# Layer 2's last projection on Trainium2: seven block products for eight

## The chip, the cores and the metric

The kernel runs on one core of one Trainium2 chip. The metric is the device time of one execution in microseconds; lower is better. TensorE does the matrix products (PE in the profile, its weight loads PEld), VectorE the elementwise work (DVE), ScalarE the activations and copies (ACT), GpSimd a few small operations (POOL), and SyncE (SP) issues most transfers. All data is fp32.

## The reference, cut to what matters

Four graph layers run one after the other on 32 independent batch elements, each with 512 nodes of 128 features and a 512x512 matrix `adj`. Every layer is `x = x + layer(relu(layernorm(x)))`. The change lies in layer 2, which has four sublayers of its own:

```
def _layer(nodes, adj, ws, bs, wd, bd, wn, bn, wu, bu):
    src = nodes @ ws + bs
    src_agg = jnp.einsum('bjv,bij->biv', src, _l2norm(adj, 2))
    dst = nodes @ wd + bd
    dst_agg = jnp.einsum('bjv,bji->biv', dst, _l2norm(adj, 1))
    self_rep = nodes @ wn + bn
    upd = jnp.concatenate([src_agg, self_rep, dst_agg], axis=2)
    return jnp.tanh(upd @ wu + bu)
...
for i in range(4):
    if i < 2:
        stashed.append(fpass)                                        # f0, f1
    elif i == 2:
        fpass = concatenate([fpass, stashed[1]], axis=2)             # f2, f1
    else:
        fpass = concatenate([fpass, stashed[1], stashed[0]], axis=2) # f3, f1, f0
    fpass = _layer(fpass, adj, *params[i])
```

The last sublayer (`i == 3`) projects three features, f3, f1 and f0, to `src` and `dst`: per element a 512x384 matrix times a 384x256 matrix. Two thirds of that product, the f1 and f0 rows of the weights, need nothing that is made after the first sublayer.

## The kernel before: the parts that matter

The program is a list of operations. Each names its engine, an estimated duration, and the buffers that it reads and writes. A list scheduler (`Plan.order`) then works out the order of instructions on every engine ahead of time, across all 32 elements, so that several elements are in flight at once. An operation's urgency comes from a due time for its element, `batch * PERIOD`, less the work that still follows. Buffers come from a fixed number of places: 8 PSUM banks, 32 places of 2 KiB a partition (`s2`), 6 of 4 KiB (`s4`), 10 of 8 KiB (`s8`).

```
plan = Plan(sb, psum, {"bank": 8, "s2": 32, "s4": 6, "s8": 10}, {"bank": 1, "s2": 7, "s4": 0, "s8": 0})
...
def t_mm(n):
    return n * 0.001675 + 0.004
def mm(ps, out_of, lhs, rhs, n, start, stop, reads, later=0.0):
    op("PE", t_mm(n), lambda: nc.tensor.matmul(out_of(ps.ap()), lhs(), rhs(), start=start, stop=stop),
       reads, [ps], later=later)
```

The last dictionary says how many places an element that isn't the oldest must leave free. All ordinary matmuls are issued in `mm`, so all of them carry the line L289 in the profile; the names of the tiles tell them apart. The helper for the source and destination projections works on two blocks of 128 nodes at a time, adds up the features in one PSUM bank, and adds the bias on VectorE (L490):

```
def paired_rows(nodes, wcols, wbuf, bias, bbuf, col):
    sd = buf("s4", (P, NC, 2 * D), "sd")
    for h in range(NC // 2):
        ps = plan.bank("sd")
        for j in range(2):
            c = 2 * h + j
            for k, nk in enumerate(nodes):
                mm(ps, lambda t, j=j: t[:, j * 2 * D:(j + 1) * 2 * D],
                   lambda nk=nk, c=c: nk.ap()[:, c * P:(c + 1) * P],
                   lambda k=k: wt(wcols + k * 2 * D, 2 * D), 2 * D, k == 0, k == len(nodes) - 1, [nk, wbuf])
        op("DVE", t_tt(N), lambda ps=ps, h=h: nc.vector.tensor_add(
            sd.ap()[:, 2 * h:2 * h + 2, :], ps.ap().rearrange("p (j v) -> p j v", j=2),
            along(bias, col, 2 * D, 2)), [ps, bbuf], [(sd, {2 * h, 2 * h + 1})])
    return sd
```

Here `P` and `D` are 128, `N` is 512 and `NC` is 4. A feature is held transposed, 128 partitions (features) by 512 columns (nodes); a 128-column block of it is the stationary operand, and the weights (128x256: source beside destination) are the moving one. The four sublayers use it like this. The weights have the update weights `wu` multiplied in once at the start ("fold"), so the aggregations add straight into the bank that the tanh reads:

```
for i, (wsd, wn) in enumerate(W_L2):
    sd = paired_rows(f, wsd, W2F, rf_sb, RF, i * 2 * D)
    ps = plan.bank("agg")
    linear_t(ps, [wn + k * D for k in range(len(f))], f, W2F, stop=False)
    for m, lo in ((aT, 0), (a, D)):
        for c in range(NC):
            mm(ps, lambda t: t, lambda c=c, lo=lo, sd=sd: sd.ap()[:, c, lo:lo + D], lambda c=c, m=m: m.ap()[:, c, :], N,
               False, lo > 0 and c == NC - 1, [(sd, {c}), (m, {c})])
    f_new = buf("s2", name=f"f{i + 1}")
    op("ACT", ...tanh of ps with bias...)
    stashed.append(f_new)
    f = {0: [f_new], 1: [f_new, stashed[1]], 2: [f_new, stashed[1], stashed[0]], 3: [f_new]}[i]
```

Of the kernel before, what the change touches and what calls it, by code (L numbers as in the profile page):

```python
# [13 lines left out]
F32 = mybir.dt.float32  # L14
# [4 lines left out]
P = 128  # L19
# [4 lines left out]
L2_CHUNKS = (1, 1, 2, 3)  # L24
PERIOD = 30.0
ENDING = 6.0
SMALL = 16


# [32 lines left out]
R_L0, R_L1_IO, R_L1_UPD, R_L3_MSG, R_L3_G, R_L3_HRZ = (k * D for k in (0, 1, 3, 4, 5, 9))  # L62
R_COLS = 11 * D

# [159 lines left out]
def gnn_stack(  # L224
# [15 lines left out]
    dram = ctx.enter_context(tc.tile_pool(name="dram", bufs=1, space=bass.MemoryType.DRAM))  # L240
    plan = Plan(sb, psum, {"bank": 8, "s2": 32, "s4": 6, "s8": 10}, {"bank": 1, "s2": 7, "s4": 0, "s8": 0})

# [3 lines left out]
    rf_sb = const.tile([P, len(L2_CHUNKS) * 2 * D], F32, name="rf_sb")  # L246
    cf_sb = const.tile([P, len(L2_CHUNKS)], F32, name="cf_sb")
    ident = const.tile([P, P], F32, name="ident")
    neg_half = const.tile([P, 2 * NC], F32, name="neg_half")
# [8 lines left out]
    def t_mm(n):  # L258
        return n * 0.001675 + 0.004

# [15 lines left out]
    def op(*args, **kwargs):  # L276
        return plan.op(*args, **kwargs)

    def const_buf(name, ap):
        b = Buf(plan, name, name, None)  # L280
        b.tile, b.slot = ap, 0
        return b

    W1, W2F, W3, CS, RS, RF, CF, ID, NH = (const_buf(n, t) for n, t in (
        ("w1", w_sb), ("w2", w_sb), ("w3", w_sb), ("c_sb", c_sb), ("r_sb", r_sb), ("rf_sb", rf_sb),
        ("cf_sb", cf_sb), ("ident", ident), ("neg_half", neg_half)))

    def mm(ps, out_of, lhs, rhs, n, start, stop, reads, later=0.0):
        op("PE", t_mm(n), lambda: nc.tensor.matmul(out_of(ps.ap()), lhs(), rhs(), start=start, stop=stop),  # L289
           reads, [ps], later=later)  # L290

    def setup():
# [5 lines left out]

        def spread(lo, hi):
            return lambda: nc.sync.dma_start(  # L300
                r_sb[:, lo:hi], bass.AP(tensor=brow.tensor, offset=brow.offset + lo, ap=[[0, P], [1, hi - lo]]))

# [7 lines left out]
        op("SP", 0.5, spread(R_L3_MSG, R_COLS), [], [(RS, {2})], kb=(R_COLS - R_L3_MSG) / 2)  # L310
        op("DVE", 0.4, lambda: nc.vector.tensor_add(r_sb[:, R_L3_G:R_L3_G + 2 * D], r_sb[:, R_L3_G:R_L3_G + 2 * D],
                                                    r_sb[:, R_L3_HRZ:R_L3_HRZ + 2 * D]), [(RS, {2})], [(RS, {2})])
        raws = []
# [12 lines left out]
        for i, (k, (proj, upd)) in enumerate(zip(L2_CHUNKS, RAW_L2, strict=True)):  # L326
# [23 lines left out]
            else:  # L350
# [4 lines left out]
            op("ACT", t_act(2 * D), lambda ps=ps, i=i: nc.scalar.copy(  # L355
                rf_sb[:, i * 2 * D:(i + 1) * 2 * D], ps.ap()[:, :2 * D]), [ps], [RF])

    def program(b):
# [119 lines left out]

        def paired_rows(nodes, wcols, wbuf, bias, bbuf, col):

            sd = buf("s4", (P, NC, 2 * D), "sd")
            for h in range(NC // 2):
                ps = plan.bank("sd")
                for j in range(2):
                    c = 2 * h + j
                    for k, nk in enumerate(nodes):
                        mm(ps, lambda t, j=j: t[:, j * 2 * D:(j + 1) * 2 * D],
                           lambda nk=nk, c=c: nk.ap()[:, c * P:(c + 1) * P],
                           lambda k=k: wt(wcols + k * 2 * D, 2 * D), 2 * D, k == 0, k == len(nodes) - 1, [nk, wbuf])
                op("DVE", t_tt(N), lambda ps=ps, h=h: nc.vector.tensor_add(  # L490
                    sd.ap()[:, 2 * h:2 * h + 2, :], ps.ap().rearrange("p (j v) -> p j v", j=2),
                    along(bias, col, 2 * D, 2)), [ps, bbuf], [(sd, {2 * h, 2 * h + 1})])
            return sd

        def tt(dst, fn, n, reads, engine="DVE"):
# [56 lines left out]
        for h in range(2):  # L552
            s, part = slice(2 * h, 2 * h + 2), {2 * h, 2 * h + 1}
            op("ACT", t_act(N), lambda s=s: nc.scalar.activation(rep.ap()[:, s, :], io.ap()[:, s, :], AF.Exp), [(io, part)], [(rep, part)])
            op("DVE", t_ts(N), lambda s=s: nc.vector.tensor_scalar(rep.ap()[:, s, :], rep.ap()[:, s, :], 1.0, -1.0, op0=ALU.min, op1=ALU.add),
               [(rep, part)], [(rep, part)])
            op("DVE", t_tt(N), lambda s=s: nc.vector.tensor_max(rep.ap()[:, s, :], rep.ap()[:, s, :], io.ap()[:, s, :]),  # L557
               [(rep, part), (io, part)], [(rep, part)])
        psi = plan.bank("agg")
# [48 lines left out]
        f0 = transposed(h2, "f0")  # L608
        f, stashed = [f0], [f0]
        for i, (wsd, wn) in enumerate(W_L2):  # L610
            sd = paired_rows(f, wsd, W2F, rf_sb, RF, i * 2 * D)
            ps = plan.bank("agg")
            linear_t(ps, [wn + k * D for k in range(len(f))], f, W2F, stop=False)
            for m, lo in ((aT, 0), (a, D)):
                for c in range(NC):
                    mm(ps, lambda t: t, lambda c=c, lo=lo, sd=sd: sd.ap()[:, c, lo:lo + D], lambda c=c, m=m: m.ap()[:, c, :], N,
                       False, lo > 0 and c == NC - 1, [(sd, {c}), (m, {c})])
            f_new = buf("s2", name=f"f{i + 1}")
            op("ACT", t_act(N, 1), lambda ps=ps, i=i, f_new=f_new: nc.scalar.activation(f_new.ap(), ps.ap(), AF.Tanh, bias=cf_sb[:, i:i + 1]),  # L619
               [ps, CF], [f_new])  # L620
            stashed.append(f_new)
            f = {0: [f_new], 1: [f_new, stashed[1]], 2: [f_new, stashed[1], stashed[0]], 3: [f_new]}[i]
        x3 = buf("s2", rows_shape, "xr")
# [27 lines left out]
        g = buf("s8", (P, NC, 4 * D), "g")  # L651
        for c in range(NC):
            ps = plan.bank("gate")
            blk = slice(c * P, (c + 1) * P)
            for m, lo, n, col, start, stop in ((h3T, 3, 1, W_L3_HH + 2 * D, True, True), (h3T, 0, 2, W_L3_HH, True, False),
                                               (mT, 0, 2, W_L3_IH, False, True), (mT, 2, 1, W_L3_IH + 2 * D, True, True)):
                mm(ps, lambda t, lo=lo, n=n: t[:, lo * D:(lo + n) * D], lambda m=m, blk=blk: m.ap()[:, blk],
                   lambda col=col, n=n: wt(col, n * D), n * D, start, stop, [m, W3], later=0.7 * c)
            op("DVE", t_tt(N), lambda ps=ps, c=c: nc.vector.tensor_add(g.ap()[:, c, :], ps.ap(), r_sb[:, R_L3_G:R_L3_G + 4 * D]),  # L659
               [ps, RS], [(g, {c})])  # L660


        u, n, q, w, xo = (buf("s2", rows_shape, k) for k in ("u", "n", "q", "w", "xo"))
        at_end = b >= B - 2
        side, side_engine = (nc.gpsimd, "POOL") if at_end else (nc.vector, "DVE")
        w1 = 1 if at_end else 2
        for k in range(0, NC, w1):
            s, part, cols = slice(k, k + w1), set(range(k, k + w1)), 2 * D * w1
            op("ACT", t_act(cols), lambda s=s: nc.scalar.activation(g.ap()[:, s, :2 * D], g.ap()[:, s, :2 * D], AF.Tanh, scale=0.5),  # L669
               [(g, part)], [(g, part)])  # L670
        w2 = 1 if at_end else NC
        for k in range(0, NC, w2):
            s, part, cols = slice(k, k + w2), set(range(k, k + w2)), w2 * D

            def step(dst, fn, reads, engine="DVE"):
                op(engine, t_tt(cols) if engine == "DVE" else t_pool(cols), fn, [(r, part) for r in reads], [(dst, part)])

            step(u, lambda s=s: nc.vector.scalar_tensor_tensor(u.ap()[:, s, :], g.ap()[:, s, 0:D], 1.0, g.ap()[:, s, 3 * D:], op0=ALU.add, op1=ALU.mult), [g])
            step(u, lambda s=s: nc.vector.scalar_tensor_tensor(u.ap()[:, s, :], u.ap()[:, s, :], 0.5, g.ap()[:, s, 2 * D:3 * D], op0=ALU.mult, op1=ALU.add), [u, g])
            op("ACT", t_act(cols), lambda s=s: nc.scalar.activation(n.ap()[:, s, :], u.ap()[:, s, :], AF.Tanh), [(u, part)], [(n, part)])  # L680
            op("ACT", t_act(cols), lambda s=s: nc.scalar.activation(w.ap()[:, s, :], g.ap()[:, s, D:2 * D], AF.Copy, scale=-0.5, bias=0.5), [(g, part)], [(w, part)])
            op("ACT", t_act(cols), lambda s=s: nc.scalar.activation(q.ap()[:, s, :], g.ap()[:, s, D:2 * D], AF.Copy, scale=0.5, bias=0.5), [(g, part)], [(q, part)])
            step(q, lambda s=s: side.tensor_tensor(q.ap()[:, s, :], q.ap()[:, s, :], h3.ap()[:, s, :], op=ALU.mult), [q, h3], side_engine)
# [55 lines left out]
```

## Time and profile before

| | us |
|---|---|
| device time, median of 3 runs | 2353.84 (2353.79 to 2356.74) |
| span of the profiled execution | 2352.6 |
| PE busy | 2321.2 |
| DVE busy | 1123.3 |
| ACT busy | 923.2 |

In the profile, a group of instructions is one line of the kernel, an engine, an operation and its tiles (output<-inputs). Times are microseconds unless marked ns. TensorE instructions are pipelined: a matmul's recorded length reaches into the next one's, so the distance between the starts of two matmuls is its price, not its length. Each fp32 matmul appears as two records.

### The profile page before, as it was taken

What the parts mean: (1) busy time and instruction counts of PE and PEld (TensorE: products, weight loads), DVE (VectorE), ACT (ScalarE), POOL (GpSimd) and SP (SyncE); (2) the same over time, 40 slices, a digit from 0 to 9 for tenths busy, and PEclk for the clock granted to TensorE, in tenths of its full rate; (3) what the DMA queues carried; (4) which work ended last, traced back from release to release, by engine and by line L of the source; (5) the groups of instructions that cost most, each with busy time, mean ns of one, the idle gap of its engine ahead of it and who ended that gap; (6) DMA issues with size and microseconds to landing.
All of it is one profiled execution on the core that took longest, in us unless ns stands there. A gap on an engine that the chain in (4) does not pass through costs nothing.

```text
span 2352.6 us, 24187 instructions
## 1 busy us (share of the span) xinstructions
PE 2321.2 (99%) x8466; PEld 1426.5 (61%) x8466; DVE 1123.3 (48%) x2917; ACT 923.2 (39%) x2018; POOL 282.0 (12%) x218
## 2 busy tenths in 40 slices
PE   6999999999999999999999999999999999999998
PEld 4665566566666565665666665656665666656655
DVE  4344444555445555445554445554455544454523
ACT  7424233443334443334443344433344333344312
POOL 3100011111011110011110111110111101111001
PEclk9999999999999999999999999999999999999999
DMA  6112212322313332223223133322233321332000
GB/s 239 59 54 72 72 52 92 108 86 88 99 56 104 90 99 90 75 78 108 90 90 99 50 103 91 98 90 82 72 107 90 98 91 55 98 107 72 17 10 9
DMA packets 127128, 196.36 MB, mean 83 GB/s; under 512 B 18336, under 2 KB 75040, under 8 KB 127008
## 3 DMA queue, kind: packets, MB, share of 16 engines
q1 hardware_dynamic: 126720, 194.71, 27.0%
q8 instruction: 66, 1.08, 0.2%
q14 instruction: 54, 0.44, 0.1%
q10 hardware_dynamic: 288, 0.13, 0.0%
HBM read 157.95 MB, written 36.83 MB: 83 GB/s over the span
## 4 chain that ended last, share of the span: by engine, by line
PE 94%; DVE 2%; ACT 2%; DMA 1%; issue 0%; POOL 0%; SPq 0%; DVEq 0%; POOLq 0%; ACTq 0%
PE ps_agg L289 62%; PE ps_sd L289 18%; PE ps_gate L289 7%; PE ps_upd L289 3%; PE ps_msg L289 1%; PE ps_lin L289 1%; PE ps_node L289 1%; ACT h L417 1%; POOL sc L405 0%; DMA a<-in_adj 0%; ACT sq L581 0%; DVE bn L389 0%; SPq L435 0%; DVE g L659 0%; DMA spaced<-bounce 0%
## 5 line engine op out<-in xcount | busy, mean ns | idle before, releaser
L289 PE MATMUL ps_agg<-aT,sd 128*128 128x512 f32 x1024 | 521.2, 593 | 0.0
L289 PE MATMUL ps_agg<-a,sd 128*128 128x512 f32 x1024 | 501.1, 592 | 0.0
L289 PE MATMUL ps_sd<-w_sb,f 128*128 128x256 f32 x1792 | 484.2, 381 | 1.0 <-ACT f L455 0.8
L490 DVE TENSOR_TENSOR sd<-ps_sd,rf_sb 128x512 f32<-128x512 f32 x256 | 175.9, 687 | 606.7 <-PE ps_sd L289 606.7
L289 PEld LDWEIGHTS ps_sd<-w_sb,f 128*128 128x128 f32 x1792 | 327.1, 191 | 172.8 <-issue 134.0
L405 POOL TENSOR_TENSOR sc<-v,neg_half 128x4 f32<-128x4 f32 (+1 forms) x128 | 180.1, 1408 | 2020.1 <-DVE v L392 1384.0
L417 ACT ACTIVATE h<-xr,nb,sc 128x128 f32<-128x128 f32 x384 | 157.9, 482 | 556.8 <-DVE nb L413 556.6
L289 PEld LDWEIGHTS ps_agg<-a,sd 128*128 128x128 f32 x1024 | 185.4, 191 | 164.3 <-issue 155.3
L289 PEld LDWEIGHTS ps_agg<-aT,sd 128*128 128x128 f32 x1024 | 187.1, 191 | 84.4 <-issue 56.9
L289 PE MATMUL ps_agg<-f,w_sb 128*128 128x512 f32 x448 | 229.7, 594 | 0.0
L619 ACT ACTIVATE f<-ps_agg,cf_sb 128x512 f32<-128x512 f32 x128 | 87.2, 681 | 132.0 <-PE ps_agg L289 131.9
L289 PE MATMUL ps_agg<-aT,rep 128*128 128x512 f32 x256 | 131.4, 595 | 3.6 <-DVE rep L557 3.6
L289 PEld LDWEIGHTS ps_gate<-w_sb,mT 128*128 128x128 f32 x512 | 95.3, 190 | 61.6 <-issue 55.0
L426 DVE STREAM_TRANSPOSE blk<-h 128x512 f32<-128x512 f32 x81 | 57.6, 711 | 154.8 <-ACT h L417 154.8
L289 PE MATMUL ps_agg<-a,rep 128*128 128x512 f32 x256 | 130.7, 592 | 0.0
L289 PE MATMUL ps_agg<-aT,msg 128*128 128x512 f32 x256 | 125.9, 592 | 0.0
L289 PE MATMUL ps_gate<-w_sb,mT 128*128 128x256 f32 (+1 forms) x512 | 123.1, 326 | 0.0
L289 PEld LDWEIGHTS ps_gate<-w_sb,hT 128*128 128x128 f32 x512 | 91.0, 190 | 49.8 <-issue 43.5
L289 PE MATMUL ps_gate<-w_sb,hT 128*128 128x128 f32 (+1 forms) x512 | 119.0, 327 | 0.0
L289 PE MATMUL ps_agg<-aT,h 128*128 128x256 f32 (+2 forms) x384 | 108.8, 380 | 0.0
L603 DVE TENSOR_TENSOR aT<-aT,rows 128x512 f32<-128x512 f32 x128 | 87.8, 687 | 35.4 <-PE ps_agg L289 33.8
L669 ACT ACTIVATE g<-g 128x512 f32<-128x512 f32 (+1 forms) x68 | 41.1, 605 | 156.1 <-DVE g L659 156.1
(101 smaller groups left out, 2724.6 us busy)
## 6 DMA issues: line engine op xcount, KB each, us to landing
aT<-in_adjt SPq DMA_DIRECT2D x124, 512.0 KB, 4.8
a<-in_adj SPq DMA_DIRECT2D x62, 512.0 KB, 4.6
turn_turned<-blk SPq DMA_DIRECT2D x324, 64.0 KB, 1.8
turned<-turn_turned SPq DMA_DIRECT2D x81, 256.0 KB, 2.6
spaced<-bounce SPq DMA_DIRECT2D x32, 512.0 KB, 4.1
x<-in_x SPq DMA_DIRECT2D x32, 256.0 KB, 2.9
out<-xo SPq DMA_DIRECT2D x30, 256.0 KB, 3.0
turn_f4r<-blk SPq DMA_DIRECT2D x108, 64.0 KB, 2.3
```

The source lines that it names most:

```text
L289: op("PE", t_mm(n), lambda: nc.tensor.matmul(out_of(ps.ap()), lhs(), rhs(), start=start, stop=stop), reads, [ps], later=later)
L405: op("POOL", t_pow(n), lambda: nc.gpsimd.tensor_tensor(inv.ap()[:, :n], v8.ap()[:, :n], neg_half[:, :n], op=ALU.pow), [v8, NH], [(inv, {0})])
L417: op("ACT", t_act(D, 2), lambda c=c: nc.scalar.activation(h.ap()[:, c, :], xin.ap()[:, c, :], AF.Relu, bias=nb.ap()[:, c:c + 1], scale=inv ...
L426: op("DVE", t_tt(N), lambda: nc.vector.transpose(blk.ap().rearrange("p b (c r) -> p c b r", c=NC), m.ap().rearrange("p c (b s) -> p c b s" ...
L490: op("DVE", t_tt(N), lambda ps=ps, h=h: nc.vector.tensor_add(sd.ap()[:, 2 * h:2 * h + 2, :], ps.ap().rearrange("p (j v) -> p j v", j=2), a ...
L603: op("DVE", t_tt(N), lambda m=m, c=c, s=s: nc.vector.tensor_mul(m.ap()[:, c, :], m.ap()[:, c, :], rows.ap()[:, s, :]), [(m, {c}), rows], [ ...
L619: op("ACT", t_act(N, 1), lambda ps=ps, i=i, f_new=f_new: nc.scalar.activation(f_new.ap(), ps.ap(), AF.Tanh, bias=cf_sb[:, i:i + 1]), [ps, ...
L669: op("ACT", t_act(cols), lambda s=s: nc.scalar.activation(g.ap()[:, s, :2 * D], g.ap()[:, s, :2 * D], AF.Tanh, scale=0.5), [(g, part)], [( ...
```

## The change

In the last sublayer the f1 and f0 parts of the projection are seen as a product of 2x2 blocks. The left matrix has the nodes in two halves (rows) and the features f1 and f0 (columns); the right one has f1's source and destination weights, and f0's below them:

```
| A11 A12 |   | b11 b12 |      A11, A21: f1, nodes 0-255 and 256-511    b11: f1 -> source   b12: f1 -> destination
| A21 A22 | * | b21 b22 |      A12, A22: f0, the same halves            b21: f0 -> source   b22: f0 -> destination
```

This takes eight block products. A scheme of Strassen's kind (Winograd's form) needs seven, for sums and differences of blocks before and after. The differences of weights don't depend on the data and are made once in the setup (`t_sb`). The purpose is less work on TensorE. The result, with the bias, goes to an `sd` buffer that is made after the first sublayer and held (`early`); the last sublayer then projects only f3 and adds the held block in the place of the bias.

Core of the diff (long parts cut; `flat2`, `region2` and `along2` are views of two node blocks):

```
-PERIOD = 30.0
+PERIOD = 28.0
+SEVEN = {"last": 0 * 5 * D}
-R_COLS = 11 * D
+R_COLS = 9 * D
-plan = Plan(..., {"bank": 1, "s2": 7, "s4": 0, "s8": 0})
+plan = Plan(..., {"bank": 1, "s2": 5, "s4": 0, "s8": 0})
+t_sb = const.tile([P, T_COLS], F32, name="t_sb")
     def t_mm(n):
-        return n * 0.001675 + 0.004
+        return n * 0.00166 + 0.0085
 ... setup: the last two of brow's blocks are loaded into a buffer of their own, hrz ...
+            combine(0, ... b12 - b11)          # t0
+            combine(1, ... b22 - t0)           # t1
+            combine(2, ... b22 - b12)          # t2
+            combine(3, ... b21 - t1)           # t3
+            combine(4, ... bias of source - bias of destination)
-        def paired_rows(nodes, wcols, wbuf, bias, bbuf, col):
+        def paired_rows(nodes, wcols, wbuf, bias, bbuf, col, sd=None):
+            held, sd = sd, sd or buf("s4", (P, NC, 2 * D), "sd")
 ...
-                    along(bias, col, 2 * D, 2)), [ps, bbuf], [(sd, {2 * h, 2 * h + 1})])
+                    sd.ap()[:, 2 * h:2 * h + 2, :] if held else along(bias, col, 2 * D, 2)), [ps, part if held else bbuf], [part])
+        def seven(site, x1, x2, dst, part):
+            H = N // 2
+            s13, s24, ev, dv, xx = (buf("s2", (P, 2, H), k) for k in ("s13", "s24", "ev", "dv", "xx"))
+            bank_a, bank_b, bank_c, bank_d = (plan.bank("seven") for _ in range(4))
+            def product(ps, k, lhs, rhs, reads):
+                for j in range(2):
+                    op("PE", t_mm(D), ... matmul(ps[:, k * H + j * D:k * H + (j + 1) * D], lhs()[:, j * P:(j + 1) * P], rhs(), start=True, stop=True), reads, [ps])
+            dve(of(s13, 1), x1 half 0, x1 half 1, sub=True)
+            product(bank_a, 0, x1 half 0, wt(b11))
+            product(bank_a, 1, of(s13, 1), t(2))
+            dve(flat2(ev, 0), region2(bank_a, 0), along2(bias of destination))
+            dve(of(ev, 1), region(bank_a, 1), of(ev, 0))
+            op("DVE", t_tt(N), ... dv = ev + t(4), both halves)
+            product(bank_d, 0, x2 half 0, wt(b21))
+            dve(of(s24, 0), x2 half 1, of(s13, 1), sub=True)
+            dve(of(s13, 0), x1 half 1, x2 half 1)
+            dve(of(s24, 1), x2 half 0, of(s24, 0), sub=True)
+            product(bank_b, 0, of(s24, 0), t(1))
+            product(bank_b, 1, of(s13, 0), t(0))
+            product(bank_c, 0, x2 half 1, t(3))
+            product(bank_c, 1, of(s24, 1), wt(b22))
+            dve(place(0, 0), region2(bank_d, 0), flat2(dv, 0))
+            op("DVE", t_tt(N), ... ev = ev + bank_b[:, :H], both halves)
+            dve(of(xx, 0), region(bank_b, 0), of(dv, 1))
+            dve(place(1, 1), region2(bank_b, 1), flat2(ev, 1))
+            dve(place(1, 0), region2(bank_c, 0), flat2(xx, 0))
+            dve(of(xx, 1), region(bank_b, 1), of(ev, 0))
+            dve(place(0, 1), region2(bank_c, 1), flat2(xx, 1))
 ... the four sublayers:
+            elif i == 3 and "last" in SEVEN:
+                sd = paired_rows(f[:1], wsd, W2F, rf_sb, RF, i * 2 * D, early)
 ... after the tanh:
+            if i == 0 and "last" in SEVEN:
+                early = buf("s4", (P, NC, 2 * D), "sd")
+                seven("last", f_new, f0, *of_halves(early))
```

The new code names two more places ("mid" and "gates") where seven products could be used. They are not in `SEVEN`, so their code isn't reached. Dependencies on `sd` and on the gates' buffer are tracked in smaller parts; the gates' matmuls and their order in the program text are as before.

## The prediction

> **What bounds the kernel now.** I read the page's busy times first, then the busy time by stretches of the run, then the waits of the tensor engine, then the order in time of a stretch from the middle.
>
> Busy times of the page, and the granted clock over the run:
>
> ```profile
> PE 2321.2 (99%) x8466; PEld 1426.5 (61%) x8466; DVE 1123.3 (48%) x2917; ACT 923.2 (39%) x2018; POOL 282.0 (12%) x218
> ...
> PEclk9999999999999999999999999999999999999999
> ```
>
> One engine fills the span, and no other is near it. But a busy tensor engine need not be a bound one, because its ends are modelled, so I look at where it idles. Busy time by stretches (start:end in us, length, then each engine's busy time):
>
> ```profile
> 0.00:20.00 20.00, 8.82 (x52) 8.11 (x53) 2.37 (x14) 12.03 (x32) 4.17 (x12) 1.00 0.88 314
> 20.00:60.00 40.00, 31.94 (x144) 21.31 (x144) 27.36 (x100) 33.80 (x90) 14.24 (x10) 0.91 0.60 204
> ...
> 1200.00:2200.00 1000.00, 998.32 (x3621) 612.37 (x3620) 494.22 (x1267) 401.65 (x870) 120.58 (x84) 1.00 0.29 87
> ...
> 2280.00:2353.00 73.00, 64.63 (x242) 40.35 (x240) 24.03 (x71) 17.15 (x48) 9.89 (x18) 0.97 0.04 11
> ```
>
> The reader is to see that the idle time sits at the two ends: 11.2 us before the first matmul and up to 20 us, 8.1 us from 20 to 60 us, 8.4 us in the last 73 us. In 1000 us of the middle it is 1.7 us. So in the middle, time is what the stream of matmuls takes to be issued, and a matmul fewer is time saved, as long as no new gap opens.
>
> What a matmul takes is not its mean duration (593 ns for 512 columns counts overlapping pieces), but the distance between starts. Each matmul shows as two records. From the order in time (start, length, operation, number of records):
>
> ```profile
> 1015.49 0.38 PE L289 MATMUL ps_upd<-w_sb,agg_in 128*128 128x128 f32 x2
> ...
> 1016.83 1.46 PE L289 MATMUL ps_sd<-w_sb,f 128*128 128x256 f32 x6
> 1018.13 1.02 PE L289 MATMUL ps_agg<-f,w_sb 128*128 128x512 f32 x2
> ...
> 1061.75 4.46 PE L289 MATMUL ps_agg<-a,sd 128*128 128x512 f32 x10
> 1066.04 0.59 PE L289 MATMUL ps_sd<-w_sb,f 128*128 128x256 f32 x2
> ...
> 1068.62 1.89 PE L289 MATMUL ps_sd<-w_sb,hT 128*128 128x256 f32 x8
> 1070.35 0.59 PE L289 MATMUL ps_sd<-w_sb,f 128*128 128x256 f32 x2
> ```
>
> Between 1015.49 and 1016.83 stand six 128-column matmuls with six different stationary blocks or weights: 1.34/6 = **0.223 us each**. Three of 256 columns take 1.30 (0.433), four take 1.73 (0.4325), and others in the trace 0.430: I take **0.432 us**. Five of 512 take 4.29: 0.858 us. The price per column is nearly even; a narrow matmul pays about 7 ns more than half of one twice as wide.
>
> The period of one batch element is seen in the chain that ended last (start, length):
>
> ```profile
> 341.00 8.59 PE ps_agg L289 x20
> 412.66 8.59 PE ps_agg L289 x20
> ```
>
> The same run of matmuls returns every 71.66 us. That is the quantity to change.
>
> [...]
>
> **The change, part by part.** Of the three features that layer 2's last projection reads, two (f1 and f0) are known long before the third.
>
> *Removed:* per batch element, 2 features x 4 row blocks = 8 matmuls of 256 columns: 8 x 0.432 = 3.456 us.
>
> *Added on the tensor engine:* seven products, each two row blocks by 128 columns: 14 x 0.223 = 3.122 us. In the order as built I count 768 instead of 1024 ps_sd matmuls and 448 new ones, so 8 and 14 for each of 32 elements.
>
> *Difference:* 3.456 - 3.122 = **0.334 us per element, 10.7 us in all**. One product of eight should have been 12.5% of 3.456, which is 0.432; 14 x 7 ns of narrowness take 0.098 back.
>
> *Added on the vector engine:* twelve additions of 256 columns [...] and two of 512 (0.687, the group of bias additions) per element: 5.09 + 1.37 = 6.5 us, 207 us in all. Busy time goes from 1123 to about 1330 us, 57% of the span. The additions of the bias stay, now adding to the held block. All this lies beside the matmuls.
>
> *Moved:* although the code makes the seven products right after the first feature, the list scheduler issues them by urgency. As built, in a middle element, they stand between the last matmuls of the third layer and the third feature's own projection. Four more banks are taken for that stretch, of eight. Between the last product and the first aggregation that needs the sum I count 0.858 x 4 + 0.432 x 3 + 0.223 = 4.95 us of other matmuls. After that product the vector engine owes two or three additions of 0.424 and the 0.687 one: 1.5 to 2.0 us plus signalling. The kernel before passes an aggregation through a 584 ns ScalarE copy with 1.7 us of matmuls between and does not wait, so 4.95 us should be ample. Counting the same distances for the other links, they are equal or longer than before (the third feature 5.6 us, earlier 2.1). So I expect no gap in the middle, and a period of 71.66 - 0.33 = 71.33 us.
>
> *Ends:* the first 60 matmul rows stand in the same order but for the place of batch 1's first aggregation. For elements 1 and 2 the first use of the sum comes only 0.9 us after its last projection, which is shorter than the 0.687 us addition plus signalling can surely meet: up to 1 us each. The last element's sum has 1.3 to 2.1 us, as the plain bias addition had before. Five more setup additions and one more small load lie beside the folding of the weights. I add 0.7 us for the ends. Sum: 2353.84 - 10.7 + 0.7 = **2343.8 us**.
>
> **Rivals.** (A) *The narrow matmuls are dearer than 0.223 us*, because 14 need weight loads where 8 did. A load is 190 ns in the trace, longer than a 128-column record's 111 ns distance[...]. For it: the waits list much "issue" time at weight loads. Against it: the ps_upd matmuls above, each with its own load, keep 0.223 in the very same stream. Break-even is 3.456/14 = 0.247 us; at that price the time stays 2354.
>
> (B) *The vector engine becomes a wait.* [...] fourteen additions come in one burst, about 8 us of work with its neighbours in 19 us of matmuls. Were the tensor engine held 1 us per element, it would lose 32 and gain 11: 2375 us. Against it: the 4.95 us above, and 57% load. Signs for it: the vector engine already waits for ps_sd and not the other way round, so lateness there has room:
>
> ```profile
> DVE sd L490 <- PE ps_sd L289: 611.6, 173, 10.7
> ```
>
> (C) *Banks and buffers.* Four banks at once plus a block held from early on could make another element's group wait for a bank, or spoil the interleaving, which the change also touches through a different period and fewer reserved buffers. Two or three microseconds at the start, or 0.1 us per element, would make 2347. (D) *The gain is hidden anyway*: excluded, as the chain is 94% tensor engine.
>
> **Range and chances.** Steady state gives -10.7 with little doubt on the price: 5 ns on the narrow matmuls would be 2.2 us. The ends can give plus or minus 3 us. Half of (B) in a few elements would take 5 us. So 8 times in 10 the time lies from 2340 to 2349 us. Faster by over 2% would need 47 us, over four times what the count gives: 1%. Slower by over 2% needs (B) at 1.8 us per element: 2%. Within 2%: 97%, and nearly all of it on the faster side.
>
> **What would show it.** The chain's repeated run should return every 71.3 us; the tensor engine should be busy over 998 us of 1000 in the middle; ps_seven should be issued at 0.223 us per matmul, with about 210 us more vector work. Wrong if: the period is 71.3 but the ends are over 3 us longer (C); ps_agg waits for sd in every element (B); or ps_seven stands 0.24 us apart (A).

## The result, and the profile after

The changed kernel takes 2337.93 us (median of 4 runs, 2336.02 to 2340.20) against 2353.82 for the kernel before (4 runs): a ratio of 0.9931, interval 0.9914 to 0.9949. That is 15.9 us less. The prediction was 2343.8 with a range from 2340 to 2349, so the direction and most of the size were right, and the gain was larger than the range allowed.

Lines have moved in the new file: ordinary matmuls are L295 (L289 before), the addition behind a projection is L523 (L490), the seven products are L567, and their additions of 256 columns L545. Busy times of the page after, and the shares of the chain that ended last:

```profile
PE 2308.9 (99%) x8850; PEld 1431.8 (61%) x8850; DVE 1271.3 (54%) x3370; ACT 947.3 (41%) x2018; POOL 255.8 (11%) x218
...
PE ps_agg L295 61%; PE ps_sd L295 14%; PE ps_gate L295 7%; PE ps_seven L567 4%; PE ps_upd L295 3%; PE ps_msg L295 1%; PE ps_lin L295 1%; PE ps_node L295 1%; ACT h L448 1%; DMA turn_f4r<-blk 0%; ACT rows L705 0%; DMA raw<-in_raw 0%; DMA f4r<-turn_f4r 0%; DVE bn L420 0%; DVE sd L523 0%
```

The same shares before:

```profile
PE ps_agg L289 62%; PE ps_sd L289 18%; PE ps_gate L289 7%; PE ps_upd L289 3%; PE ps_msg L289 1%; PE ps_lin L289 1%; PE ps_node L289 1%; ACT h L417 1%; POOL sc L405 0%; DMA a<-in_adj 0%; ACT sq L581 0%; DVE bn L389 0%; SPq L435 0%; DVE g L659 0%; DMA spaced<-bounce 0%
```

The tensor engine is still the bound: ps_sd fell from 18% of the chain to 14%, and ps_seven has 4%. Busy time by stretches, the columns as in the prediction (PE, PEld, DVE, ACT and POOL; then the granted clock of the tensor engine, where 1.00 is full, and the DMA share and GB/s):

```profile
20.00:60.00 40.00, 31.83 (x153) 22.14 (x152) 27.45 (x105) 34.81 (x93) 15.00 (x11) 0.91 0.56 195
...
1200.00:2200.00 1000.00, 998.72 (x3812) 617.98 (x3811) 561.81 (x1467) 402.75 (x843) 101.44 (x81) 1.00 0.28 85
```

The middle has no new gap. The repeated run of the chain:

```profile
928.50 5.15 PE ps_agg L295 x12
999.82 5.15 PE ps_agg L295 x12
```

It returns after 71.32 us; 71.33 was predicted, 71.66 was before. And the new matmuls in order of time:

```profile
1037.98 0.38 PE L567 MATMUL ps_seven<-t_sb,f 128*128 128x128 f32 x2
1038.20 0.39 PE L567 MATMUL ps_seven<-w_sb,f 128*128 128x128 f32 x2
1038.43 0.39 PE L567 MATMUL ps_seven<-w_sb,s 128*128 128x128 f32 x2
1038.65 0.60 PE L295 MATMUL ps_sd<-w_sb,f 128*128 128x256 f32 x2
```

They stand 0.22 to 0.23 us apart. So what was predicted per element came true, and yet 5 us more were gained than the count gives. To find them I took all matmul records of a trace, and for each the distance to the next start less the usual distance of its width (111, 216, 323 and 429 ns a record for 128, 256, 384 and 512 columns, 109 for a transpose: the medians of the kernel before). The sum of these usual distances is the price of the work; the sum of what is over is the time that the tensor engine lost. The price fell by 32 x (16 x 0.216 - 28 x 0.111) = 11.1 us.

Lost time is not all waiting. At the start the tensor engine runs for a while at half its clock: the granted clock reads 0.50 for 6.8 us from 51.9 us on in the kernel before, and for 6.8 us from 48.8 us on in the repeat of the changed one. From the kernel before, two rows in that stretch:

```profile
56.21 1.06 PE L289 MATMUL ps_sd<-w_sb,f 128*128 128x256 f32 x2
57.06 1.84 PE L289 MATMUL ps_agg<-aT,sd 128*128 128x512 f32 x2
```

A matmul of 256 columns takes 0.85 us there from start to start, where 0.432 is its price. The first matmuls, ahead of the first clock reading at some 14 to 16 us, stand about twice as far apart too: records of 128 columns (ps_fold) start 213 to 215 ns apart in the kernel before and in the changed one, where 111 is usual. The last column of the table is the part of the loss that is due to such doubled distances; the rest is waiting.

| time lost, us | 0 to 200 us | 200 to 2200 | after 2200 | all | of it, doubled distances |
|---|---|---|---|---|---|
| kernel before | 18.1 | 6.0 | 2.7 | 26.8 | 4.4 |
| changed kernel, first profile | 16.5 | 6.0 | 1.5 | 24.0 | 4.7 |
| changed kernel, profile of the repeat | 15.8 | 4.6 | 1.5 | 21.9 | 4.0 |
| before, three numbers only | 16.1 | 10.5 | 1.6 | 28.1 | 3.8 |
| before, period 28 only | 14.4 | 10.6 | 2.0 | 27.0 | 3.1 |
| changed, period 30 | 19.0 | 23.3 | 1.8 | 44.0 | 6.3 |
| changed, reserve 7 | 16.4 | 36.4 | 3.6 | 56.4 | 5.4 |
| changed, all three old numbers | 18.3 | 82.7 | 10.9 | 111.9 | 15.5 |
| early, but eight plain products | 21.0 | 28.4 | 1.8 | 51.2 | 8.4 |
| changed, additions twice | 18.5 | 24.2 | 4.4 | 47.1 | 6.9 |
| changed, one product twice | 16.3 | 4.8 | 1.5 | 22.6 | 4.2 |
| third sublayer too, rightly paired | 17.2 | 7.0 | 1.9 | 26.1 | 4.3 |

(Rows are sums of rounded parts.) The repeat's span is 16.7 us shorter than that of before: 11.1 price, 4.9 lost time, and 0.6 in which the first weights landed earlier (10.5 us, 11.1 before). The first profile's span is 14.2 us shorter, and its lost time 2.8. The first profile is of the longest of its four executions and the repeat's of the shortest of its five, so 2.8 to 4.9 us is what the traces show beyond the price; the medians of the times say 4.8 and 4.9. Doubled distances have no part in this (0.4 us less in the repeat, 0.3 more in the first profile).

### The profile page after: what moved, and what is told of

The parts are those of the page before. It is cut to its first block, busy times and chain, and to the rows that moved or that the text cites. A ratio compares the mean times of both kernels' runs of the same rounds, so it can differ in the third digit from the quotient of the medians.

```text
span 2338.4 us, 25489 instructions
## 1 busy us (share of the span) xinstructions
PE 2308.9 (99%) x8850; PEld 1431.8 (61%) x8850; DVE 1271.3 (54%) x3370; ACT 947.3 (41%) x2018; POOL 255.8 (11%) x218
## 4 chain that ended last, share of the span: by engine, by line
PE 93%; DVE 3%; ACT 2%; DMA 1%; issue 0%; POOL 0%; SPq 0%; DVEq 0%; POOLq 0%; ACTq 0%
PE ps_agg L295 61%; PE ps_sd L295 14%; PE ps_gate L295 7%; PE ps_seven L567 4%; PE ps_upd L295 3%; PE ps_msg L295 1%; PE ps_lin L295 1%; PE ps_node L295 1%; ACT h L448 1%; DMA turn_f4r<-blk 0%; ACT rows L705 0%; DMA raw<-in_raw 0%; DMA f4r<-turn_f4r 0%; DVE bn L420 0%; DVE sd L523 0%
## 5 line engine op out<-in xcount | busy, mean ns | idle before, releaser
L295 PE MATMUL ps_agg<-aT,sd 128*128 128x512 f32 x1024 | 512.2, 593 | 0.2 <-DVE sd L523 0.2
L295 PE MATMUL ps_agg<-a,sd 128*128 128x512 f32 x1024 | 511.1, 593 | 0.0
L295 PE MATMUL ps_sd<-w_sb,f 128*128 128x256 f32 x1280 | 373.3, 381 | 1.4 <-ACT f L486 0.7
L436 POOL TENSOR_TENSOR sc<-v,neg_half 128x4 f32<-128x4 f32 (+1 forms) x128 | 150.7, 1178 | 1900.9 <-DVE v L423 1837.7
L295 PEld LDWEIGHTS ps_sd<-w_sb,f 128*128 128x128 f32 x1280 | 227.1, 191 | 138.7 <-issue 108.6
L295 PEld LDWEIGHTS ps_agg<-aT,sd 128*128 128x128 f32 x1024 | 180.9, 191 | 100.2 <-issue 89.9
L295 PE MATMUL ps_agg<-f,w_sb 128*128 128x512 f32 x448 | 229.7, 594 | 0.0
L295 PEld LDWEIGHTS ps_agg<-a,sd 128*128 128x128 f32 x1024 | 176.8, 191 | 83.2 <-issue 76.6
L523 DVE TENSOR_TENSOR sd<-ps_sd,rf_sb 128x512 f32<-128x512 f32 x192 | 130.8, 682 | 150.8 <-PE ps_sd L295 150.6
L800 DVE TENSOR_TENSOR g<-ps_gate,r_sb 128x512 f32<-128x512 f32 x128 | 80.5, 684 | 148.6 <-PE ps_agg L295 135.4
L448 ACT ACTIVATE h<-x,nb,sc 128x128 f32<-128x128 f32 x128 | 53.1, 482 | 235.9 <-DVE nb L444 235.8
L295 PEld LDWEIGHTS ps_gate<-w_sb,mT 128*128 128x128 f32 x512 | 91.4, 190 | 73.2 <-issue 69.1
L295 PE MATMUL ps_agg<-aT,rep 128*128 128x512 f32 x256 | 130.7, 593 | 1.6 <-DVE rep L663 1.6
L295 PE MATMUL ps_agg<-a,rep 128*128 128x512 f32 x256 | 130.4, 592 | 0.0
L295 PE MATMUL ps_agg<-aT,msg 128*128 128x512 f32 x256 | 130.2, 593 | 0.0
L523 DVE TENSOR_TENSOR sd<-ps_sd,sd 128x512 f32<-128x512 f32 x64 | 44.2, 691 | 151.3 <-PE ps_sd L295 151.3
L705 ACT COPY rows<-spaced 128x1024 f32<-128x1024 f32 x32 | 65.8, 2055 | 149.0 <-DMA spaced<-bounce 147.5
L295 PE MATMUL ps_gate<-w_sb,mT 128*128 128x256 f32 (+1 forms) x512 | 118.6, 327 | 0.0
L295 PEld LDWEIGHTS ps_gate<-w_sb,hT 128*128 128x128 f32 x512 | 87.0, 191 | 48.5 <-issue 43.5
L295 PE MATMUL ps_gate<-w_sb,hT 128*128 128x128 f32 (+1 forms) x512 | 114.7, 327 | 0.0
```

The source lines that it names most:

```text
L436: op("POOL", t_pow(n), lambda: nc.gpsimd.tensor_tensor(inv.ap()[:, :n], v8.ap()[:, :n], neg_half[:, :n], op=ALU.pow), [v8, NH], [(inv, {0})])
L448: op("ACT", t_act(D, 2), lambda c=c: nc.scalar.activation(h.ap()[:, c, :], xin.ap()[:, c, :], AF.Relu, bias=nb.ap()[:, c:c + 1], scale=inv ...
L523: op("DVE", t_tt(N), lambda ps=ps, h=h: nc.vector.tensor_add(sd.ap()[:, 2 * h:2 * h + 2, :], ps.ap().rearrange("p (j v) -> p j v", j=2), s ...
L705: op("ACT", t_act(2 * N), lambda: nc.scalar.copy(rows.ap().rearrange("p s (c n) -> p (s c) n", c=NC), spaced.ap().rearrange("p n k -> p k ...
```

## The experiments

The theories. P: the gain is the price of the matmuls alone. E: price, and a few us at the two ends of the run. For E, the cause could be the scheduler's three numbers (the period of the due times, the reserve of buffers, the estimate of a matmul) or the held block; a third part of the change, the finer tracking of dependencies, was not tried alone. Intervals are 95% intervals of the ratio to the kernel before, taken in the same session. The rivals of the prediction, dear narrow matmuls (A) and a waiting vector engine (B), are tried too.

**The changed kernel again**, with no edit.

> The changed kernel once more, with more runs. Theory P (the matmuls' price alone, 8 x 2 x 0.216 less 14 x 2 x 0.111 us for each of 32 elements): 11.1 us below the kernel before, so near 2342.7. Theory E (price, and 3 to 5 us more from shorter gaps at the two ends of the run): 2337 to 2340.

Measured: 2339.07 us (5 runs), before 2355.07, ratio 0.9931, interval 0.9919 to 0.9944. P is out: 16.0 us are gained (13 to 19 by the interval), not 11.1. That more than the price is gained holds; where it lies, the table tells.

**The three numbers alone**, in the kernel before:

```
-PERIOD = 30.0                              +PERIOD = 28.0
-{"bank": 1, "s2": 7, "s4": 0, "s8": 0}     +{"bank": 1, "s2": 5, "s4": 0, "s8": 0}
-return n * 0.001675 + 0.004                +return n * 0.00166 + 0.0085
```

> The kernel before with only the scheduler's three numbers of the change (due-time period 28 for 30, 5 reserved places for 7, the new estimate of a matmul); no seven products. If the part beyond the price comes from these numbers: 2349 to 2351. If it comes from the held block or is scatter: 2353 to 2354.5.

Measured: 2359.34 us, ratio 1.0024, interval 1.0014 to 1.0034. Neither line was met: it is slower. The table tells a part of why: the ends do lose 3.1 us less, 0.6 of it doubled distances, but the middle loses 4.5 us more. That makes 1.3 of the 4.3 us between the medians; the profile is of the shortest of the nine executions (2355.23 us), and what the others lose isn't traced. The waits of its tensor engine (us in total, times, longest):

```profile
PE ps_sd L289 <- ACT f L619: 4.0, 8, 0.9
```

This is the projection waiting for a sublayer's feature, now and then. In the changed kernel's repeat this kind of wait is 0.3 us.

**The seven products with the three old numbers** (the same edit backwards, in the changed kernel).

> The changed kernel with the scheduler's three numbers of before. If these numbers bring the part beyond the price: 2342 to 2343.5. If the seven products and the held block bring it: 2337 to 2340.

Measured: 2427.29 us, ratio 1.0302, interval 1.0288 to 1.0316. Far outside both: the work saved is the same, and the kernel is 88 us slower than the changed one. Its waits:

```profile
PE ps_sd L295 <- ACT f L489: 39.7, 23, 3.4
PE ps_sd L295 <- ACT hT L489: 12.9, 21, 1.2
```

The repeat has neither among its waits. L489 copies a transposed feature of a younger element out of the buffer in which a transfer has put it. In 23 elements that feature comes up to 3.4 us late. By starts, 46 gaps ahead of `ps_sd` matmuls make 63 of the 83 us lost in the middle. The granted clock also falls to 0.50 seven times after the start, which costs 11.5 us in doubled distances (its mean over the run is 0.992, for 0.998 in the repeat). So the numbers are not a detail of the change.

**The two features early, with plain products:**

```
-early = buf("s4", (P, NC, 2 * D), "sd")
-seven("last", f_new, f0, *of_halves(early))
+early = paired_rows([f_new, f0], W_L2[3][0] + 2 * D, W2F, rf_sb, RF, 3 * 2 * D)
```

> The changed kernel with the first two features projected early by eight 256-column matmuls in place of the seven products, held and added in the same way. The tensor engine's stream is then that of before. If the price is all that the products bring and the rest comes from schedule or holding: 2349 to 2351. If neither holding nor schedule brings anything: 2353 to 2354.5.

Measured: 2376.02 us, ratio 1.0083, interval 1.0070 to 1.0097. The matmul stream has the price of before, but the order has a gap in nearly every element:

```profile
PE ps_lin L295 <- ACT agg L633: 20.7, 25, 2.0
```

Holding the block early brings nothing by itself in this order. It isn't a clean measure of holding, since the order changed all over.

**The three numbers one at a time**, each in the changed kernel: reserve 7, period 30, old estimate.

> The changed kernel with 7 reserved places for 5 and nothing else; five new half-filled buffers per element then meet a tighter store. If the reserve is what cost the kernel with all three old numbers its 88 us: 2400 to 2430. If not: 2335 to 2345.

> The changed kernel with due times 30 us apart for 28 and nothing else. If the due times cost the 88 us: 2400 to 2430. If not: 2335 to 2345.

> The changed kernel with the old estimate of a matmul (128 columns: 0.2184 for 0.2210 us, 512: 0.8616 for 0.8584) and nothing else. If this estimate cost the 88 us: 2400 to 2430. If not: 2335 to 2345.

Measured: 2372.08 us (ratio 1.0074, interval 1.0059 to 1.0089), 2361.44 us (1.0023, 1.0014 to 1.0032) and 2338.24 us (0.9928, 0.9911 to 0.9944). The estimate does nothing. The reserve costs 33 us and the period 22; together, in the run with all three, 88, so they make each other worse. What I expected, that one of them would carry the whole, was wrong. The period's cost is the cleanest gap of the study. Its waits, and one instance in order of time (the bracket holds the idle time and what ended it):

```profile
PE ps_agg L295 <- DVE sd L523: 12.3, 24, 0.6
```

```profile
1001.09 1.03 PE L295 MATMUL ps_sd<-w_sb,f 128*128 128x256 f32 x4
1002.64 0.70 PE L295 MATMUL ps_agg<-aT,sd 128*128 128x512 f32 x1 [0.52 <-DVE sd L523]
```

Two projections that fill the same bank are issued in a row, and the aggregation stands directly behind them: nothing lies between to cover the addition. By starts, the second row comes 1.55 us after the first, where 0.86 would be its turn: 0.68 us here, 16.3 us in the 25 elements that have this gap, and 2.6 more because the first record behind it is 0.1 us slow. Some 3 us of the rest are lost in the first 200 us, 2.3 of them in doubled distances.

**The twelve 256-column additions twice**, in the same order of instructions:

```
-op("DVE", t_tt(H), lambda: nc.vector.tensor_tensor(o(), a(), b(), ...), reads, writes)
+def twice():
+    for _ in range(2):
+        nc.vector.tensor_tensor(o(), a(), b(), ...)
+op("DVE", t_tt(H), twice, reads, writes)
```

> The changed kernel, every engine's order kept, but each of the twelve 256-column additions is issued twice in a row (same result): about 5 us more vector work for each element, 160 us in all. If the vector engine's additions lie beside the matmuls with room (the prediction): 2337 to 2343. If they are close to being a wait (rival B): 5 us or more for each element in part or whole, 2360 to 2500.

Measured: 2360.63 us, ratio 1.0028, interval 1.0016 to 1.0040; 22 us more than the changed kernel. The page's busy times:

```profile
PE 2320.6 (98%) x8850; PEld 1431.5 (61%) x8850; DVE 1421.5 (60%) x3754; ACT 948.2 (40%) x2018; POOL 256.6 (11%) x218
```

150 us more vector work cost 22 us, a seventh. The largest piece is one link, here in the order of the tensor engine and of the vector engine (L667 is L663 of the changed kernel):

```profile
1290.40 1.02 PE L295 MATMUL ps_agg<-a,sd 128*128 128x512 f32 x2
1291.56 1.12 PE L295 MATMUL ps_agg<-aT,rep 128*128 128x512 f32 x2
```

```profile
1290.82 0.68 DVE L667 TENSOR_TENSOR rep<-rep,sd 128x512 f32<-128x512 f32 x1
```

The aggregation comes 1.16 us after the row ahead of it, where 0.86 would be its turn, and 0.06 us after the vector engine ended `rep`. This happens 24 times and costs 7.2 us, with the slow record behind it 9.7; 2.9 us more than in the repeat are doubled distances, and the rest is scattered. So the additions do lie beside the matmuls, as predicted, but with less room than I claimed: at a load of only 60% they already make other operations of the vector engine late. This is a part of rival B. As the kernel stands, the tensor engine's wait for an addition of the block (ps_agg for sd) is 0.2 us in one profile and under the shortest listed in the other.

**One product twice**, in the same order:

```
+for _ in range(2 if ps is bank_a and k == 0 else 1):
     nc.tensor.matmul(...)
```

> The changed kernel, every engine's order kept, with one of the seven products (f1's first half by b11, two matmuls of 128 columns) issued twice: 64 matmuls more. If a narrow matmul costs its distance between starts, 0.222 us, on the path: 14.2 us more than the changed kernel, 2352 to 2354. If part of it is hidden in gaps: less. If weight loads make it dearer (rival A, 0.247 us): 15.8 or more, from 2355.

Measured: 2352.95 us; 13.9 more than the changed kernel's 2339.07, or 0.217 us for each of 64 matmuls. The page counts 8978 weight loads for 8850, so each of them has its own loads, and the time lost stays (22.6 us, 21.9 in the repeat). A narrow matmul costs its distance between starts, one for one. Rival A (0.247 us) is out, by the starts above more clearly than by these medians alone, which have some us of scatter.

**The due times alone**, in the kernel before: `PERIOD = 28.0`.

> The kernel before with due times 28 us apart for 30 and nothing else. If the due times are what shortens the first 60 us (numbers-only kernel: 12.4 us of gaps there for 13.8): the same here, with 2352 to 2360 in all, the middle deciding. If the reserve is what shortens it: 13.8 us of gaps there as before.

Measured: 2354.45 us, ratio 0.9998, interval 0.9989 to 1.0006. Time lost from 20 to 60 us is 12.2 us, for 13.8 before and 12.4 in the repeat, which looks like the answer. But the granted clock of that stretch is 0.96 here and 0.91 before:

```profile
20.00:60.00 40.00, 31.57 (x151) 21.69 (x150) 26.45 (x100) 34.73 (x90) 15.18 (x11) 0.96 0.57 201
```

The reading of 0.50 lasts 3.4 us in this trace and 6.8 in that of before, and this makes 1.4 of the 1.6 us; the waits there are 10.7 and 10.9 us. What the due times do remove are waits between 60 and 201 us, 2.2 us of them, 1.3 in a single gap at 200 us. In the stream of before the middle takes it back (10.6 for 6.0 us).

**The third sublayer too.** The code has a second place prepared; only the table changes: `SEVEN = {"last": 0, "mid": 5 * D}`.

> The changed kernel with the seven products used in the third sublayer's projection of f2 and f1 too, a place that the code has prepared; these cannot be made early. Price alone: another 11.1 us less, 2327 to 2329. If the vector engine's further 6.5 us per element, or the chain from f2 over products and additions to the aggregation, opens a gap: 2340 to 2380.

Measured: 2329.93 us, ratio 0.9899, interval 0.9884 to 0.9914. As prepared, this place multiplies f1 by the rows of f2's weights and the other way round, so it does the same work on other columns and its time alone is of use. The next run has them paired rightly:

```
+order = (2, 3, 0, 1) if site == "mid" else (0, 1, 2, 3)
-return [at + k * D for k in range(4)], ...
+return [at + k * D for k in order], ...
```

> As the run with the third sublayer's seven products, but with the two features paired with their own weights; instructions and orders are the same, only the weight columns read differ. Price alone for both places, 22.2 us below the kernel before, and the shorter ends of the changed kernel, 4 to 5: 2328 to 2331. If the earlier time hung on the data or the weights: outside that.

Measured: 2330.37 us against 2354.30 for before, ratio 0.9895, interval 0.9878 to 0.9911. This is the fastest version of the study that computes the reference's function. Its chain:

```profile
925.26 5.15 PE ps_agg L295 x12
996.25 5.15 PE ps_agg L295 x12
```

The period is 70.99 us, another 0.33 less. Of the 10.6 us that this is worth over 32 elements some 8 arrive (23.9 us below the kernel before, 16.0 for the repeat): its trace loses 1.4 us more than the repeat's at the start and 2.4 more in the middle.

## Why the prediction was right and wrong, by its own steps

*Price.* Right. 10.7 us were predicted and 11.1 are found; I took 0.223 us for a narrow matmul, and the medians make it 0.222. The period was right to 0.01 us, and doubling a product confirms that the price is paid in full.

*No gap in the middle.* Right for this order: 4.6 and 6.0 us lost in 2000 us, 6.0 before. The counted distances (4.95 us from the last product to the aggregation, 5.6 us behind the third feature) were a good guide.

*Vector engine.* Right that it lies beside, with less room than claimed. Mis-sized: 148 us more busy time, not 207. The new additions last about what I took, 201 us by their groups: for one of 256 columns I took 0.424 us (twelve of them are the 5.09 us), and their groups have means from 403 to 425 ns, with a median of 415 over all 384. The only one in the kernel before, in the setup, lasts 420 ns. But another group was recorded with 27 us less,

```profile
L413 DVE SCALAR_TENSOR_TENSOR nb<-mv,sc 128x4 f32<-128x4 f32 x128 | 50.0, 391 | 94.1 <-POOL sc L405 93.8
```

```profile
L444 DVE SCALAR_TENSOR_TENSOR nb<-mv,sc 128x4 f32<-128x4 f32 x128 | 22.7, 178 | 73.5 <-POOL sc L436 69.4
```

and records overlap by 30 us more, which the busy time counts once (193 us of overlap after, 163 before; see the last section). Why `nb` is shorter stays open.

*Ends.* This is the step that failed: "I add 0.7 us for the ends." In the traces the lost time falls instead, by 2.8 us (first profile) to 4.9 (repeat): 1.7 to 2.4 us in the first 200, 1.2 after 2200, and 0 to 1.4 between. I had compared the order of the first 60 matmul rows, seen little difference, and looked only for new waits of the new block. I did not ask what a new order, with another period and reserve, would do to gaps that the kernel before already had. In its waits there were such gaps to lose, and I had them in hand:

```profile
PE ps_agg L289 <- DVE rep L557: 3.6, 3, 1.5
PE ps_msg L289 <- ACT hT L458: 1.3, 1, 1.3
```

After, the first is 1.6 us, once, and the second is gone: 3.3 us in three gaps, or 4.1 by starts. They stood at 200, 283 and 2099 us, where the first elements fill the kernel and the last ones empty it; some small new gaps take a part back. The three numbers without any new product shorten the waits at the two ends by 2.6 us. Which part of the change removes which gap is not shown.

*The rivals.* (C) came closest, with the wrong sign. I named the period and the reserve, and put them at 2 or 3 us of loss. A choice of these numbers is worth far more: with the old ones the same products make the kernel 3% slower than before. That the new ones came with the change is why no such loss showed; the prediction did not derive it. My 2% for "slower" and the narrow range were too sure of an order that I had checked only at a few links.

*Still open.* Why a reserve of 7 makes features late in the changed kernel. That five more buffers per element starve the younger ones is likely, and the waits on L489 fit it, but no run shows it. Why the granted clock falls for 3.4 us in one trace and 6.8 in another isn't shown either. A version that makes the products after the third feature wasn't tried.

## What to carry to other kernels

Where one engine is busy 99% of the time, price the change by that engine's distances between starts: it comes out to a few per cent of the gain. Then treat the order of instructions as a part of the change. When it is made by a list scheduler, re-tune its numbers with every change of the work: here they decide over 16 us of gain or 72 us of loss, while the work saved is worth 11. Read the waits that the kernel already has, since a new order can remove them as well as add some. And before a gap is put down to the order, look at the granted clock of its stretch: here a stretch that looked better ordered had only been at half clock for less time.

## What the runs showed of the hardware that I had not expected

Vector additions in a row start closer together than they last. In the run with the additions twice (L547 is L545 of the changed kernel):

```profile
1285.89 0.88 DVE L547 TENSOR_TENSOR s<-f 128x256 f32<-128x256 f32 x2
1286.69 0.88 DVE L547 TENSOR_TENSOR s<-f,f 128x256 f32<-128x256 f32 x2
```

```profile
1288.08 0.68 DVE L823 SCALAR_TENSOR_TENSOR u<-g 128x512 f32<-128x512 f32 x1
1288.68 0.68 DVE L828 TENSOR_TENSOR q<-q,h 128x512 f32<-128x512 f32 x1
```

For 512 columns the start (first column) moves by 0.60 us where each is recorded with 0.68 (second column). Two of 256 columns took 0.80 us from the first start to the next operation, 0.40 each, where one lasts 0.42. So in such a row a sum of recorded durations overstates the vector engine's load, as it does for matmuls.
